# Attention on one core: the next image's pieces in other rounds, keys of two heads in one row tile, and the exponentials' sums right behind the scores

## The chip, the core and the metric

The kernel runs on one core of a Trainium2 chip. Its time is the device time of one launch in microseconds (us), here the median of several runs. The engines are TensorE (PE in the profile; its weight loads are PEld), VectorE (DVE), ScalarE (ACT), GpSimd (POOL) and SyncE (SP, which issues the DMAs). Each takes its own instructions in order and waits for others by semaphores. Matmuls write to PSUM; a PSUM tile of 128 x 512 float32 is called a bank here.

## What is computed

The whole is a block of two layers over eight images of 128 channels and 32 x 32 places: attention, a spectral filter, a deformable convolution and a mixture of experts, each behind a norm and added to its input. The change lies in the first of them, cut here to what matters:

```python
x = x + attention(layer_norm_over_channels(x), wq, wk, wv)      # 8 images
# in attention, per image: 1024 tokens of 128 channels, 8 heads of 16
q, k, v = (xp @ w.T for w in (wq, wk, wv))
weights = softmax(einsum('bhwnd,bxynd->bnhwxy', q, k) * 16 ** -0.5)
out = einsum('bnhwxy,bxynd->bhwnd', weights, v)
```

All is float32. The scores are bounded beforehand, so that the softmax needs no maximum: exponential, sum, division.

## The kernel before, in words

`metaformer_kernel` first prepares image 0 (`BoundedAttention.tokens` and `.matrices`) and then calls `attention_bounded`, lines 495 to 755, which does all eight images. The later stages (`Spectral`, `DeformAndExperts`) follow on the same engines; the change doesn't touch them.

**Units and rounds.** A unit is a quarter of an image's queries (256) with four of its eight heads (a head group, `hg`): eight units per image, 64 in all. A unit has four rounds `r`, and each round takes two of the eight key tiles. The work is written as a list of entries (round, order in the round, function), sorted, and issued in that order; each engine's queue is then the order of its own instructions in that list. A unit that begins at round `t0` is spread over twelve rounds, so that three units overlap:

- rounds `t0` to `t0+3`, order 0, `scores` (L596): eight matmuls (as the profile counts, 16 passes) of 32 rows by 128 columns, one for each head and key tile, into `s`, which takes four PSUM banks and has one buffer; then ScalarE's exponential of all of it into `e` (L609). Order 1, `add_tiles` (L615): GpSimd adds the two key tiles of `e` into `t`.
- round `t0+5`, order 4, `sums` (L621): matmuls with `group` add `t` over groups of partitions into `z`; order 5, `reciprocals` (L630) on VectorE.
- round `t0+6`, order 2.5, `spread_out` (L634): matmuls spread the reciprocals over the partitions again, into `rb`; rounds `t0+6` to `t0+9`, order 3, `divide` (L644): VectorE multiplies `e` by `rb`.
- rounds `t0+8` to `t0+11`, `values` (L650): matmuls with the values' tiles into `av`. The second tile is split between the end of `t0+8` and `t0+9`.
- every second unit: `take` (L664) copies `av`, and `results` (L668) turns it back with two matmuls by `pick`, copies it, and GpSimd adds it to the image's tokens `xt`.

Since units begin at rounds divisible by four, the same kinds of work meet in all rounds of one number modulo 4.

**The next image.** Between these stand the pieces that prepare the next image, by lists of round numbers (L698 to L731): `load` its channels, `tokens` (L533, transposes into `xt`), 25 pieces of the layer norm (`layer_norm_pieces`, L66: eight of statistics on VectorE, nine of the inverse deviation on GpSimd, two small operations each, eight normalisations on ScalarE into `ht`), `channels` (L543, transposes of `ht` into `hk`), and the projections: `keys` (L569) and `queries` (L555), one matmul of 128 x 512 for each head group and half image, and `key_values` (L582). All small matmul results, `z` among them, go through one PSUM bank (`small_bank`, L527), and ScalarE copies them out (VectorE reads `z`).

**Layout of the heads.** Head `4 hg + j` has row tile `j` (32 rows) of head group `hg`; its 16 channels fill the first half of the tile, the rest is zero, for queries and keys alike. So keys exist once for each head group.

The lists of rounds as they stand, for image 2 and later (`first` is the image's first round):

```python
project_at = [first + n for n in (-13, -12, -9, -5, -4, -1, 3, 4, 7, 11)]
turn = {"channels": (first - 20, first - 17)}
turn.update(load=first - 42, tokens=(first - 38, first - 34))
norm_at = [first - n for n in (
    37, 36, 35, 34, 33, 32, 32, 31, *range(31, 22, -1), 22, 22, 22, 21, 19, 19, 18, 18)]
```

Of the kernel before, what the change touches and what calls it, by code (L numbers as in the profile page):

```python
# [18 lines left out]
P = 128  # L19
# [380 lines left out]
class BoundedAttention:  # L400
# [6 lines left out]
    def __init__(self, nc, cp):  # L407
        self.nc = nc
        HG, NH = self.HG, self.NH
        self.xc = cp.tile([P, T], F32, name="xc")  # L410
        self.ht = cp.tile([P, NT, C], F32, name="ht")
        self.hk = cp.tile([P, T], F32, name="hk")
        self.wq, self.wk = (cp.tile([P, HG, NH, 32], F32, name=n) for n in ("wq", "wk"))
        self.wv = cp.tile([C, C], F32, name="wv")
        self.group = cp.tile([P, NG], F32, name="group")
        self.spread = cp.tile([P, 2, P], F32, name="spread")
        self.pick = cp.tile([P, HG, NH, HD], F32, name="pick")

    def keys_view(self):
        return self.hk.rearrange("c (r p) -> c r p", p=P)  # L420

    def tokens(self, x, ident, pool, ps):

        nc = self.nc
        nc.sync.dma_start(self.xc, x[0].rearrange("c h w -> c (h w)"))
        xv = self.xc.rearrange("c (i p two) -> c two i p", two=2, p=P)
        st = pool.tile([P, NT, 6], F32, name="f_st")
        mv = pool.tile([P, NT, 2], F32, name="f_mv")
        banks = []
        for par in range(2):  # L430
            pt = ps.tile([P, 4, P], F32, tag="x", name="p_x")
            for i in range(4):
                nc.tensor.transpose(pt[:, i, :], xv[:, par, i, :], ident)
            banks.append(pt)
            for i in range(4):
                nc.vector.bn_stats(st[:, 4 * par + i, :], pt[:, i, :])
                nc.vector.bn_aggr(mv[:, 4 * par + i, :], st[:, 4 * par + i, :])
        rs = inverse_std(nc, pool, mv[:, :, 1], 1e-6, nc.vector)
        for par in range(2):
            for i in range(4):  # L440
                n = 4 * par + i
                nc.vector.tensor_scalar(
                    self.ht[:, n, :], banks[par][:, i, :], mv[:, n, 0:1], rs[:, n : n + 1],
                    ALU.subtract, ALU.mult,
                )
# [3 lines left out]
            nc.scalar.copy(  # L449
                self.keys_view()[:, 4 * par : 4 * par + 4, :].rearrange(  # L450
                    "c r (g m) -> c r g m", m=4
                ),
                pb.rearrange("c i p -> c (i p)").rearrange("c (g r m) -> c r g m", r=4, m=4),
            )

    def matrices(self, wqT, wkT, wvT):
        nc, HG, NH = self.nc, self.HG, self.NH
        for w, src in ((self.wk, wkT), (self.wq, wqT)):
            nc.gpsimd.memset(w, 0.0)
            for hg in range(HG):  # L460
                nc.sync.dma_start(
                    w[:, hg, :, 0:HD],
                    src[:, hg * NH * HD : (hg + 1) * NH * HD].rearrange("c (h d) -> c h d", d=HD),
                )
        nc.sync.dma_start(self.wv, wvT)

        group = self.group
        nc.gpsimd.memset(group, 1.0)
# [15 lines left out]
            )  # L484


        nc.gpsimd.memset(self.pick, 0.0)
        for hg in range(HG):
            nc.gpsimd.affine_select(
                out=self.pick[:, hg], in_=self.pick[:, hg], pattern=[[-32, NH], [-1, HD]],  # L490
                base=-HD * hg, channel_multiplier=1, compare_op=ALU.not_equal, fill=1.0,
            )


def attention_bounded(ctx, tc, ident, x, x1d, given, weigh, head):


# [8 lines left out]
    QU = 256  # L506
    QC = T // QU
    UNITS = HG * QC
    wq, wk, wv = given.wq, given.wk, given.wv
    group, spread, pick = given.group, given.spread, given.pick  # L510
    hk = given.keys_view()
    cp = ctx.enter_context(tc.tile_pool(name="a_const", bufs=1))
    sb = ctx.enter_context(tc.tile_pool(name="a_sb", bufs=2))
    ep = ctx.enter_context(tc.tile_pool(name="a_e", bufs=11))
# [25 lines left out]
        xt = img["xt"][:, par * 4 : par * 4 + 4, :]  # L540
        nc.scalar.copy(xt.rearrange("p a c -> p (a c)"), pt)

    def channels(par):  # L543
# [6 lines left out]
        nc.scalar.copy(  # L550
            hk[:, 4 * par : 4 * par + 4, :].rearrange("c r (g m) -> c r g m", m=4),
            pt.rearrange("c (g r m) -> c r g m", r=4, m=4),
        )

    def queries(img, hg, par):  # L555
# [3 lines left out]
        nc.tensor.matmul(  # L559
            pq, wq[:, hg].rearrange("c h d -> c (h d)"),  # L560
            hk[:, 4 * par : 4 * par + 4, :].rearrange("c r p -> c (r p)"),
            start=True, stop=True,
        )
        nc.scalar.copy(
            img["q"][:, hg, par, :].rearrange("p (g r m) -> p r g m", r=4, m=4),
            pq.rearrange("p (r g m) -> p r g m", r=4, m=4),
        )

    def keys(img, hg, par):  # L569
        if "k" not in img:  # L570
            img["k"] = sb.tile([P, HG, NT, P], F32, tag="k", name="k")
        pk = small_bank("pk")
        nc.tensor.matmul(  # L573
            pk, wk[:, hg].rearrange("c h d -> c (h d)"),
            hk[:, 4 * par : 4 * par + 4, :].rearrange("c r p -> c (r p)"),
            start=True, stop=True,
        )
        nc.scalar.copy(
            img["k"][:, hg, 4 * par : 4 * par + 4, :].rearrange("p c n -> p (c n)"), pk
        )  # L580

    def key_values(b, img, par):  # L582
        pv = small_bank("pv")
        for r in range(4):
            nc.tensor.matmul(
                pv[:, r * P : (r + 1) * P], hk[:, 4 * par + r, :], wv,
                start=True, stop=True,
            )
        img["v"] = vts[b % 2]
# [6 lines left out]
    def scores(img, un, r):  # L596
# [4 lines left out]
        for c in range(2):  # L601
            for j in range(NH):
                rows = slice(32 * j, 32 * j + 32)
                nc.tensor.matmul(  # L604
                    s[:, j, c, :], img["k"][rows, hg, 2 * r + c, :],
                    q[rows, qc * QU : (qc + 1) * QU], start=True, stop=True,
                )
        e = ep.tile([P, NH, 2, QU], F32, tag="e", name="e")
# [59 lines left out]
    def results(b, img, qc, qrt):  # L668
# [1 line left out]
            img["at"] = sb.tile([P, NT, C], F32, tag="at", name="at", bufs=1)  # L670
        po = small_bank("po")
        for i in range(2):
            nc.tensor.matmul(  # L673
                po[:, i * P : (i + 1) * P], qrt["o"][:, i * P : (i + 1) * P],
                pick.rearrange("p g j d -> p (g j d)"), start=True, stop=True,
            )
        nc.scalar.copy(
            img["at"][:, 2 * qc : 2 * qc + 2, :].rearrange("p i c -> p (i c)"), po[:, 0 : 2 * P]
# [16 lines left out]
    for b in range(B):  # L695
        img = {}
        first = 4 * UNITS * b
        project = [  # L698
            (keys, img, 0, 0), (keys, img, 0, 1), (queries, img, 0, 0),
            (keys, img, 1, 0), (keys, img, 1, 1), (queries, img, 1, 0),  # L700
            (key_values, b, img, 0), (key_values, b, img, 1),
            (queries, img, 0, 1), (queries, img, 1, 1),
        ]
        if b == 0:
            turn = {"tokens": (0, 0)}
            project_at = (-1, -1, -1, 0, 1, 2, 3, 4, 7, 11)
        else:
            project_at = [first + n for n in (-13, -12, -9, -5, -4, -1, 3, 4, 7, 11)]
            turn = {"channels": (first - 20, first - 17)}
            if b == 1:  # L710
                turn.update(load=0, tokens=(2, 3))
                norm_at = (3, 3, 4, 4, 5, 5, 6, 6) + (6, 7, 7, 8, 8, 8, 9, 9, 9) + (
                    10, 10, 10, 11, 13, 13, 14, 14)
            else:
                turn.update(load=first - 42, tokens=(first - 38, first - 34))
                norm_at = [first - n for n in (
                    37, 36, 35, 34, 33, 32, 32, 31, *range(31, 22, -1), 22, 22, 22, 21, 19, 19, 18, 18
                )]
        if b:
            at(turn["load"], 6, load, b)  # L720
            spread_rounds(
                layer_norm_pieces(nc, sb, lambda i=img: i["xt"], lambda: given.ht, 1e-6), norm_at
            )
            for par in range(2):
                at(turn["channels"][par], 5.5, channels, par)
# [6 lines left out]
        for qc in range(QC):  # L732
            qrt = {}
            for hg in range(HG):
                un = {"at": (qc, hg)}
                t0 = first + 4 * (HG * qc + hg)
                for r in range(4):
                    at(t0 + r, 0, scores, img, un, r)
                    at(t0 + r, 1, add_tiles, un, r)
                    at(t0 + 5, 4, sums, un, r)  # L740
                    at(t0 + 6 + r, 3, divide, un, r)
                at(t0 + 8, 2, values, img, un, 0, (0, 1), qrt)
                at(t0 + 8, 6.5, values, img, un, 1, (0,), qrt)
                at(t0 + 9, 2, values, img, un, 1, (1,), qrt)
                at(t0 + 10, 2, values, img, un, 2, (0, 1), qrt)
                at(t0 + 11, 2, values, img, un, 3, (0, 1), qrt)
                at(t0 + 5, 5, reciprocals, un)
                at(t0 + 6, 2.5, spread_out, un)
# [1491 lines left out]
```

## Time and profile before

| | us |
|---|---|
| runs, median (lowest to highest of 3) | 1886.62 (1885.5 to 1890.1) |
| profiled execution | 1886.46 |
| its span | 1884.7 |
| busy: TensorE, VectorE, GpSimd, ScalarE over the span | 1682.4, 1389.0, 1157.9, 1064.8 |
| busy in the attention stage, 0 to 905 us: TensorE, VectorE, GpSimd, ScalarE | 863.5, 715.6, 665.7, 588.0 |
| one exponential (L609), 256 of them, mean | 1.88 |
| one division (L646), 256 of them, mean | 2.28 |
| one sum of two tiles (L618), 256 of them, mean | 2.38 |
| one reciprocal (L632), 64 of them, mean | 1.76 |

The profile is of one execution. In it, "busy" is the time in which an engine has an instruction under way; matmuls overlap with each other, so that a busy TensorE need not be at its peak. Behind an arrow stands the instruction that ended an engine's wait. The chain of waits is the work that ended last, followed backwards from the last instruction: it tells at each moment what the end of the whole was waiting for. A row's name is the tile that is written and, behind the arrow, the tiles that are read, with the line of the kernel.

### The profile page before, as it was taken

The page shows a single profiled execution, that of the slowest core. Times are in us where ns is not written, and L with a number is a line of the kernel's source. Part 1 is how long each engine was busy: PE and PEld are TensorE (multiplying, and loading weights), DVE is VectorE, ACT ScalarE, POOL GpSimd, SP SyncE. Part 2 cuts the span into 40 slices and gives each one's busy share as a digit, 9 for nine tenths or more (in the row PEclk, how much of TensorE's full clock was granted, in tenths as well). Part 3 has the DMA queues.
Part 4 walks back from the last instruction along what each step waited for, and adds up shares of the span by engine and source line. Part 5 has one row for each costly group of instructions (what it writes and reads, how often), then busy time and mean ns, then how long its engine had stood idle before and what let it go on. Part 6 is the DMA issues. An engine that isn't in the chain of part 4 may idle for free.

```text
span 1884.7 us, 51873 instructions
## 1 busy us (share of the span) xinstructions
PE 1682.4 (89%) x22324; PEld 1033.1 (55%) x22324; DVE 1389.0 (74%) x2107; ACT 1064.8 (56%) x1692; POOL 1157.9 (61%) x1219
## 2 busy tenths in 40 slices
PE   6899999999999999998577899999888497888788
PEld 3455555555555555554233688888665264555555
DVE  3688787878888888888544666666148888999883
ACT  3666666676766667666234455555145655666630
POOL 3778777777878777787221244345126768888740
PEclk9999999999999999999788999999899687999999
DMA  1000000000000000000658322122568775755620
GB/s 30 13 2 24 2 2 24 2 24 2 24 2 24 2 2 24 2 13 2 143 142 242 129 71 71 48 71 59 179 194 263 237 213 153 234 174 164 205 81 21
DMA packets 157998, 156.15 MB, mean 83 GB/s; under 512 B 15424, under 2 KB 136864, under 8 KB 156352
## 3 DMA queue, kind: packets, MB, share of 16 engines
q1 hardware_dynamic: 142400, 102.41, 19.1%
q0 software_dynamic: 15360, 50.34, 8.5%
q8 instruction: 176, 2.88, 0.6%
q14 instruction: 62, 0.51, 0.1%
HBM read 96.39 MB, written 56.33 MB: 81 GB/s over the span
## 4 chain that ended last, share of the span: by engine, by line
PE 60%; DVE 16%; issue 7%; POOL 6%; ACT 4%; DMA 2%; SPq 2%; DVEq 0%; ACTq 0%; POOLq 0%
PE s L604 14%; PE av L656 13%; PE p_g L1958 6%; PE z L625 6%; PE p_z L2007 5%; PE rb L639 4%; PE p_out L1420 3%; DVE ga L1410 3%; DVE g L1317 2%; ACT e L609 2%; PE pq L559 2%; PE pk L573 2%; POOL g L1295 1%; DVE zs L2019 1%; PE po L673 1%
## 5 line engine op out<-in xcount | busy, mean ns | idle before, releaser
L618 POOL TENSOR_TENSOR t<-e 128x1024 f32<-128x1024 f32 x256 | 608.2, 2376 | 204.7 <-ACT e L609 204.4
L646 DVE TENSOR_TENSOR e<-e,rb 128x2048 f32<-128x2048 f32 x256 | 570.4, 2278 | 84.5 <-PE rb L639 84.5
L609 ACT ACTIVATE e<-s 128x2048 f32<-128x2048 f32 x256 | 481.0, 1879 | 255.1 <-PE s L604 252.0
L604 PE MATMUL s<-q,k 32*128 32x256 f32 x4096 | 295.2, 402 | 14.6 <-ACT e L609 13.8
L656 PE MATMUL av<-e,vt 128*32 128x256 f32 x4096 | 287.4, 388 | 4.8 <-DVE e L646 3.5
L1295 POOL DMA_INDIRECT g<-tab,idx x192 | 200.3, 1043 | 134.1 <-ACT cn_m L1515 66.8
L604 PEld LDWEIGHTS s<-q,k 32*128 32x128 f32 x4096 | 185.9, 185 | 137.8 <-ACT e L609 116.9
L1302 ACT ACTIVATE g<-g,w 128x128 f32<-128x128 f32 x604 | 186.4, 390 | 57.0 <-DMA g<-tab,idx 43.2
L1983 POOL TENSOR_SCALAR at<-uc 128x256 f32<-128x256 f32 (+2 forms) x62 | 75.4, 1219 | 173.4 <-PE p_z L2007 128.9
L656 PEld LDWEIGHTS av<-e,vt 128*32 128x32 f32 x4096 | 101.1, 109 | 141.5 <-issue 83.8
L1958 PE MATMUL p_g<-v,a 32*128 32x128 f32 x4096 | 159.3, 284 | 9.4 <-ACT ga L1690 3.7
L632 DVE RECIPROCAL r<-z 128x256 f32<-128x256 f32 x64 | 112.5, 1758 | 70.4 <-PE z L625 70.2
L1958 PEld LDWEIGHTS p_g<-v,a 32*128 32x128 f32 x4096 | 132.3, 186 | 38.3 <-issue 23.0
L1420 PE MATMUL p_out<-ga,ew 128*128 128x512 f32 x256 | 127.5, 645 | 15.5 <-DVE ga L1410 15.4
L625 PE MATMUL z<-t,group 128*32 128x256 f32 x2048 | 122.2, 379 | 0.0
L1692 DVE COPY gb<-p_g 128x512 f32<-128x512 f32 x128 | 82.4, 685 | 46.7 <-PE p_g L1958 46.1
L1692 DVE COPY ga<-p_g 128x512 f32<-128x512 f32 x128 | 82.4, 686 | 44.0 <-PE p_g L1958 44.0
L1690 ACT COPY gb<-p_g 128x512 f32<-128x512 f32 x128 | 68.7, 589 | 69.6 <-PE p_g L1958 68.8
L1690 ACT COPY ga<-p_g 128x512 f32<-128x512 f32 x128 | 68.7, 589 | 66.7 <-PE p_g L1958 66.7
L1410 DVE TENSOR_TENSOR ga<-p_g,tc 128x2048 f32<-128x2048 f32 x32 | 73.0, 2282 | 29.5 <-PE p_g L1401 29.5
L1420 PEld LDWEIGHTS p_out<-ga,ew 128*128 128x128 f32 x256 | 50.1, 205 | 75.6 <-issue 56.2
L625 PEld LDWEIGHTS z<-t,group 128*32 128x32 f32 x2048 | 66.4, 110 | 44.1 <-issue 0.3
(312 smaller groups left out, 2421.3 us busy)
## 6 DMA issues: line engine op xcount, KB each, us to landing
tab<-hx SPq DMA_DIRECT2D x24, 512.0 KB, 5.8
tab<-hx SPq DMA_DIRECT2D x72, 128.0 KB, 5.3
ud<-us SPq DMA_DIRECT2D x8, 1024.0 KB, 5.3
uc<-ud SPq DMA_DIRECT2D x16, 512.0 KB, 4.0
yd<-zs SPq DMA_DIRECT2D x32, 256.0 KB, 3.2
ga<-yd SPq DMA_DIRECT2D x32, 256.0 KB, 3.8
xc<-in_x SPq DMA_DIRECT2D x8, 512.0 KB, 3.9
x1d<-xt SPq DMA_DIRECT2D x8, 512.0 KB, 2.9
```

The costliest lines, as they stand in the source:

```text
L604: nc.tensor.matmul(s[:, j, c, :], img["k"][rows, hg, 2 * r + c, :], q[rows, qc * QU : (qc + 1) * QU], start=True, stop=True,)
L609: nc.scalar.activation(e.rearrange("p j c q -> p (j c q)"), s.rearrange("p j c q -> p (j c q)"), AF.Exp, scale=float(HD) ** -0.5,)
L618: nc.gpsimd.tensor_add(t, e[:, :, 0, :], e[:, :, 1, :])
L625: nc.tensor.matmul(un["z"][32 * j : 32 * j + 32, 0:QU], group, un["t", r][:, j, :], start=(r == 0), stop=(r == 3), skip_group_check=True,)
L646: nc.vector.tensor_tensor(e, e, un["rb"].unsqueeze(2).to_broadcast([P, NH, 2, QU]), ALU.mult)
L656: nc.tensor.matmul(qrt["av"][32 * j : 32 * j + 32, 0:QU], img["v"][:, 2 * r + c, P * hg + 32 * j : P * hg + 32 * j + 32], un["e", r][:, j, ...
L1295: nc.gpsimd.indirect_dma_start(out=t["g", i][:, tap].rearrange("p k c -> p (k c)"), out_offset=None, in_=rows, in_offset=bass.IndirectOffs ...
L1302: nc.scalar.activation(t["g", i][:, tap, k, :], t["g", i][:, tap, k, :], AF.Identity, scale=t["w"][:, i, tap, k : k + 1],)
L1420: nc.tensor.matmul(t["out"], self.ew[:, first + e, :], xg[:, e, :], start=(first + e == 0), stop=(first + e == NE - 1), skip_group_check=True,
L1690: self.nc.scalar.copy(dst, src)
L1692: self.nc.vector.tensor_copy(dst, src)
L1958: nc.tensor.matmul(banks[j][:, i * P : (i + 1) * P], self.a[rows, 4 * n + i, :], self.v[rows, ch].rearrange("p f k -> p (f k)"), start=Tru ...
```

## The change

It does five things, all in the attention stage.

1. Heads are laid out in another way: head `2 j + hg` has row tile `j`. A row tile of the keys now holds two heads, 16 rows each, and serves both head groups; the queries of head group `hg` keep zeros in the other head's rows. There is one key projection for half an image instead of two, and the key tile is half as large. The values' matrix is reordered in the same way, and since the results then come out in the order of the channels, `results` uses transposes by the identity instead of matmuls by `pick`, which goes.
2. `hk`, the turned channels, has two buffers, taken in turn by image.
3. `sums` goes from order 4 to order 1.5 of its round: behind the scores, ahead of values, spread and divisions.
4. The second half of the second value tile goes from round `t0+9` to `t0+10`, ahead of `spread_out`; the third value tile goes behind `spread_out` (order 2.7).
5. The pieces of the next image go to other rounds. All projections now lie in rounds of number 3 modulo 4, tokens, channels and results in those of number 0 (with exceptions in images 0 and 1), the statistics in those of number 1, and the inverse deviation is done in four rounds with two or three pieces each.

```diff
-        self.hk = cp.tile([P, T], F32, name="hk")
-        self.wq, self.wk = (cp.tile([P, HG, NH, 32], F32, name=n) for n in ("wq", "wk"))
-        self.wv = cp.tile([C, C], F32, name="wv")
+        self.hk = [cp.tile([P, T], F32, name=f"hk{n}") for n in range(2)]
+        self.wq = cp.tile([P, HG, NH, 32], F32, name="wq")
+        self.wk = cp.tile([C, C], F32, name="wk")
+        self.wv = cp.tile([C, HG, NH, HD], F32, name="wv")
...
-        for w, src in ((self.wk, wkT), (self.wq, wqT)):
-            nc.gpsimd.memset(w, 0.0)
-            for hg in range(HG):
-                nc.sync.dma_start(
-                    w[:, hg, :, 0:HD],
-                    src[:, hg * NH * HD : (hg + 1) * NH * HD].rearrange("c (h d) -> c h d", d=HD),
-                )
-        nc.sync.dma_start(self.wv, wvT)
+        nc.sync.dma_start(self.wk, wkT)
+        nc.gpsimd.memset(self.wq, 0.0)
+        for hg in range(HG):
+            at = slice(HD * hg, HD * hg + HD)
+            nc.sync.dma_start(
+                self.wq[:, hg, :, at], wqT.rearrange("c (h n) -> c h n", n=2 * HD)[:, :, at]
+            )
+            nc.sync.dma_start(
+                self.wv[:, hg], wvT.rearrange("c (h n) -> c h n", n=2 * HD)[:, :, at]
+            )
...
-        nc.gpsimd.memset(self.pick, 0.0)
-        for hg in range(HG):
-            nc.gpsimd.affine_select(
-                out=self.pick[:, hg], in_=self.pick[:, hg], pattern=[[-32, NH], [-1, HD]],
-                base=-HD * hg, channel_multiplier=1, compare_op=ALU.not_equal, fill=1.0,
-            )
...
-    def keys(img, hg, par):
+    def keys(b, img, par):
         if "k" not in img:
-            img["k"] = sb.tile([P, HG, NT, P], F32, tag="k", name="k")
+            img["k"] = sb.tile([P, NT, P], F32, tag="k", name="k")
...
-                    s[:, j, c, :], img["k"][rows, hg, 2 * r + c, :],
+                    s[:, j, c, :], img["k"][rows, 2 * r + c, :],
...
-            nc.tensor.matmul(
-                po[:, i * P : (i + 1) * P], qrt["o"][:, i * P : (i + 1) * P],
-                pick.rearrange("p g j d -> p (g j d)"), start=True, stop=True,
+            nc.tensor.transpose(
+                po[:, i * P : (i + 1) * P], qrt["o"][:, i * P : (i + 1) * P], ident
             )
...
         project = [
-            (keys, img, 0, 0), (keys, img, 0, 1), (queries, img, 0, 0),
-            (keys, img, 1, 0), (keys, img, 1, 1), (queries, img, 1, 0),
+            (keys, b, img, 0), (keys, b, img, 1), (queries, b, img, 0, 0), (queries, b, img, 1, 0),
             (key_values, b, img, 0), (key_values, b, img, 1),
-            (queries, img, 0, 1), (queries, img, 1, 1),
+            (queries, b, img, 0, 1), (queries, b, img, 1, 1),
         ]
+        project_at = [first + n for n in (-13, -9, -5, -1, 3, 7, 11, 15)]
         if b == 0:
             turn = {"tokens": (0, 0)}
-            project_at = (-1, -1, -1, 0, 1, 2, 3, 4, 7, 11)
+            project_at = (-1, -1, -1, 3, 4, 7, 11, 15)
+        elif b == 1:
+            turn = {"load": 0, "tokens": (8, 12), "channels": (18, 20)}
+            norm_at = (9, 9, 10, 10, 13, 13, 14, 14) + (14, 14, 15, 15, 15, 15, 16, 16, 16) + (
+                17, 17, 17, 17, 18, 18, 19, 19)
         else:
...
+            turn = {
+                "load": first - 42, "tokens": (first - 36, first - 28),
+                "channels": (first - 20, first - 12),
+            }
+            norm_at = [first - n for n in (35, 35, 31, 31, 27, 27, 27, 27)] + [
+                first - n for n in (26, 26, 25, 25, 24, 24, 23, 23, 23)
+            ] + [first - n for n in (22, 22, 21, 21, 19, 18, 15, 14)]
...
-                    at(t0 + 5, 4, sums, un, r)
+                    at(t0 + 5, 1.5, sums, un, r)
                     at(t0 + 6 + r, 3, divide, un, r)
                 at(t0 + 8, 2, values, img, un, 0, (0, 1), qrt)
                 at(t0 + 8, 6.5, values, img, un, 1, (0,), qrt)
-                at(t0 + 9, 2, values, img, un, 1, (1,), qrt)
-                at(t0 + 10, 2, values, img, un, 2, (0, 1), qrt)
+                at(t0 + 10, 2, values, img, un, 1, (1,), qrt)
+                at(t0 + 10, 2.7, values, img, un, 2, (0, 1), qrt)
```

More of the change, by code (lines that the diff above doesn't have):

```diff
@@ L411, in __init__, with keys_view @@
         self.ht = cp.tile([P, NT, C], F32, name="ht")
-        self.hk = cp.tile([P, T], F32, name="hk")
-        self.wq, self.wk = (cp.tile([P, HG, NH, 32], F32, name=n) for n in ("wq", "wk"))
-        self.wv = cp.tile([C, C], F32, name="wv")
+        self.hk = [cp.tile([P, T], F32, name=f"hk{n}") for n in range(2)]
+        self.wq = cp.tile([P, HG, NH, 32], F32, name="wq")
+        self.wk = cp.tile([C, C], F32, name="wk")
+        self.wv = cp.tile([C, HG, NH, HD], F32, name="wv")
         self.group = cp.tile([P, NG], F32, name="group")
         self.spread = cp.tile([P, 2, P], F32, name="spread")
-        self.pick = cp.tile([P, HG, NH, HD], F32, name="pick")
-    def keys_view(self):
-        return self.hk.rearrange("c (r p) -> c r p", p=P)
+    def keys_view(self, b):
+        return self.hk[b % 2].rearrange("c (r p) -> c r p", p=P)
     def tokens(self, x, ident, pool, ps):
@@ L449, in tokens @@
             nc.scalar.copy(
-                self.keys_view()[:, 4 * par : 4 * par + 4, :].rearrange(
+                self.keys_view(0)[:, 4 * par : 4 * par + 4, :].rearrange(
                     "c r (g m) -> c r g m", m=4
@@ L508, in attention_bounded @@
     UNITS = HG * QC
-    wq, wk, wv = given.wq, given.wk, given.wv
-    group, spread, pick = given.group, given.spread, given.pick
-    hk = given.keys_view()
+    wq, wk, wv = given.wq, given.wk, given.wv.rearrange("c g j d -> c (g j d)")
+    group, spread = given.group, given.spread
     cp = ctx.enter_context(tc.tile_pool(name="a_const", bufs=1))
@@ L541, in tokens, with channels @@
         nc.scalar.copy(xt.rearrange("p a c -> p (a c)"), pt)
-    def channels(par):
+    def channels(b, par):
         pt = small_bank("pb")
@@ L550, in channels, with queries @@
         nc.scalar.copy(
-            hk[:, 4 * par : 4 * par + 4, :].rearrange("c r (g m) -> c r g m", m=4),
+            given.keys_view(b)[:, 4 * par : 4 * par + 4, :].rearrange(
+                "c r (g m) -> c r g m", m=4
+            ),
             pt.rearrange("c (g r m) -> c r g m", r=4, m=4),
         )
-    def queries(img, hg, par):
+    def queries(b, img, hg, par):
         if "q" not in img:
@@ L560, in queries @@
             pq, wq[:, hg].rearrange("c h d -> c (h d)"),
-            hk[:, 4 * par : 4 * par + 4, :].rearrange("c r p -> c (r p)"),
+            given.keys_view(b)[:, 4 * par : 4 * par + 4, :].rearrange("c r p -> c (r p)"),
             start=True, stop=True,
@@ L567, in queries @@
         )
[L569 removed]
+    def keys(b, img, par):
         if "k" not in img:
[L571 removed]
+            img["k"] = sb.tile([P, NT, P], F32, tag="k", name="k")
         pk = small_bank("pk")
         nc.tensor.matmul(
[L574 to L575 removed]
+            pk, wk, given.keys_view(b)[:, 4 * par : 4 * par + 4, :].rearrange("c r p -> c (r p)"),
             start=True, stop=True,
@@ L578, in keys @@
         nc.scalar.copy(
-            img["k"][:, hg, 4 * par : 4 * par + 4, :].rearrange("p c n -> p (c n)"), pk
+            img["k"][:, 4 * par : 4 * par + 4, :].rearrange("p c n -> p (c n)"), pk
         )
@@ L585, in key_values @@
             nc.tensor.matmul(
-                pv[:, r * P : (r + 1) * P], hk[:, 4 * par + r, :], wv,
+                pv[:, r * P : (r + 1) * P], given.keys_view(b)[:, 4 * par + r, :], wv,
                 start=True, stop=True,
@@ L698, in attention_bounded @@
         project = [
-            (keys, img, 0, 0), (keys, img, 0, 1), (queries, img, 0, 0),
-            (keys, img, 1, 0), (keys, img, 1, 1), (queries, img, 1, 0),
+            (keys, b, img, 0), (keys, b, img, 1), (queries, b, img, 0, 0), (queries, b, img, 1, 0),
             (key_values, b, img, 0), (key_values, b, img, 1),
-            (queries, img, 0, 1), (queries, img, 1, 1),
+            (queries, b, img, 0, 1), (queries, b, img, 1, 1),
         ]
+        project_at = [first + n for n in (-13, -9, -5, -1, 3, 7, 11, 15)]
         if b == 0:
             turn = {"tokens": (0, 0)}
-            project_at = (-1, -1, -1, 0, 1, 2, 3, 4, 7, 11)
-        else:
[L708 to L718, printed above, removed]
+            project_at = (-1, -1, -1, 3, 4, 7, 11, 15)
[3 more added lines that the diff above has]
+                17, 17, 17, 17, 18, 18, 19, 19)
+        else:
+            turn = {
[5 more added lines that the diff above has]
+            ] + [first - n for n in (22, 22, 21, 21, 19, 18, 15, 14)]
         if b:
@@ L724, in attention_bounded @@
             for par in range(2):
-                at(turn["channels"][par], 5.5, channels, par)
+                at(turn["channels"][par], 5.5, channels, b, par)
         for par in range(2):
```

## Prediction

> **What bounds the kernel now.** I read the page's slices first, then the busy time by stage, then the chain of waits round by round, then the order of time on all engines. The change touches only the attention stage, which runs from 0 to about 905 us; behind it the order of instructions on every engine is the same in both kernels, so the rest is taken as unchanged. By stage, TensorE is busy 109.5 of every 110 us between 160 and 820 us (clock 1.00), VectorE 91, GpSimd 85, ScalarE 75. That looks like a plain TensorE bound, but the chain says more. Its columns are start, length, what:
>
> ```profile
> 415.41 1.07 PE s L604 x16
> 416.48 0.57 PE av L656 x8
> 417.05 1.73 PE z L625 x32
> 418.78 1.08 PE s L604 x16
> 419.86 1.00 PE av L656 x16
> 420.86 1.06 PE rb L639 x8
> 421.92 1.13 PE s L604 x16
> 423.05 1.00 PE av L656 x16
> 424.05 1.05 PE pk L573 x2
> 425.11 1.09 PE s L604 x16
> 426.19 1.00 PE av L656 x16
> 427.19 1.05 PE pk L573 x2
> 428.25 0.57 PE av L656 x8
> ```
>
> These are four rounds, one unit's period. Call them by their number modulo 4: round 1 (scores, half of the second value tile, sums) takes 3.37 us, round 2 (scores, values, spread reciprocals) 3.14, round 3 (scores, values, a projection) 3.19, round 0 (scores, values, a piece, half a value tile) 3.71. Every scores group is followed at once by other matmuls. What happens where TensorE has less to do stands near the end of the last image, which has no projections:
>
> ```profile
> 850.14 1.15 PE L604 MATMUL s<-q,k 32*128 32x256 f32 x16 [1.00 <-ACT e L609]
> ...
> 851.38 1.88 ACT L609 ACTIVATE e<-s 128x2048 f32<-128x2048 f32 x1 [0.92 <-PE s L604]
> ...
> 853.31 1.15 PE L604 MATMUL s<-q,k 32*128 32x256 f32 x16 [0.59 <-ACT e L609]
> ```
>
> Scores have one buffer of four PSUM banks. The exponential starts 1.24 us after its scores, takes 1.88, and the next scores start 0.05 later: 3.17 us is a floor of every round, set by the loop scores, exponential, scores. So a round takes the larger of 3.17 us and its TensorE work, and slack of one round can't be carried into the next, since TensorE is in order and the next scores wait for this exponential. This decides the case: TensorE work taken from a round above 3.17 counts, taken from one at 3.17 it doesn't, and moved into a round already full it costs all of it.
>
> Check on before: round 0 with results 3.30 (four an image), with keys 3.73 (two), with values' projection 3.74, with turned channels 3.25, sum 27.65; round 1, 8 x 3.38 = 27.0; round 2, 6 x 3.17 + 2 x 3.81 (with the next image's tokens) = 26.6; round 3, 8 x 3.17 = 25.4. Total 106.65; measured from scores to scores at the same place of two images (276.30 to 382.90 us) 106.6.
>
> **The change part by part, one image in the middle.**
> Round 1 loses the half value tile: 1.07 + 1.73 = 2.8 us of work, so 3.17 by the floor: 8 x (3.17 - 3.38) = -1.7.
> Round 2 gains it: scores 1.07, half tile 0.57, spread 1.06, values 1.00: 3.70 us of TensorE work against 3.14. Spread must also wait for the reciprocal. At the start the trace shows sums right behind scores, as the change makes them everywhere:
>
> ```profile
> 55.13 1.15 PE L604 MATMUL s<-q,k 32*128 32x256 f32 x16 [0.94 <-ACT e L609]
> ...
> 58.21 1.76 DVE L632 RECIPROCAL r<-z 128x256 f32<-128x256 f32 x1 [10.34 <-PE z L625]
> ...
> 60.02 0.73 PEld L639 LDWEIGHTS rb<-r,spread 64*128 64x128 f32 x8 [0.95 <-DVE r L632]
> ```
>
> That is 4.89 us from round 1's scores to spread; minus the round's 3.17 it is 1.72 into round 2, where TensorE is ready at 1.64. So 3.70 us if the wait vanishes, 3.78 if not; I take 3.78, since this is the very sequence. 8 x (3.78 - 3.17) = +4.9, and -1.3 more for the two tokens that leave round 2 (3.81 to the other rounds' 3.17).
> A rule weighs on this part. The Trainium skill ("TensorEngine Tiling (Array Packing)", Key Properties) says that a change of tiling mode drains TensorE. The rows agree in kind: eight value matmuls cost 0.57 and sixteen 1.00, not twice 0.50. The new round 2 goes scores, values, spread, values, scores: one mode change more than before per unit. By pure count the half tile would be 0.50 and the round 3.63 (0.07 x 64 = 4.5 us less in the whole); I keep the rows, which hold the drain.
> Round 0: results become transposes. The chain has four turned-channel transposes at 0.59, so two take about 0.3, where two matmuls with the pick matrix took 0.64; 2.94 us of work, so 3.17: 4 x -0.13 = -0.5. Keys and values' projection move out: 2 x -0.56 and -0.57, minus 1.7. Tokens (0.68) move in, 1.07 + 1.00 + 0.68 + 0.57 = 3.32 twice: +0.3; turned channels 3.24 twice (one came from round 3): +0.1.
> Round 3 carries all eight projections, 1.07 + 1.00 + 1.05 = 3.12, under the floor: nothing. Two of four key projections (1.05 us and a copy of 0.59 each) are gone from the image, but they are worth only what is counted in round 0.
> Sum: 12.7 + 6.64 + 6.48 (round 0), 25.36, 30.24, 25.36 = 106.8 against 106.6: +0.15. The 3.5 us less TensorE work is eaten by round 2.
>
> **Norm pieces on GpSimd.** Before, the inverse deviation was spread one piece of two small operations per round. Now it is two, two, two and three pieces in rounds 26 to 23 before the image, and ScalarE's first two normalisations stand in round 22 before it, in ScalarE's queue ahead of round 21's exponential. GpSimd has the tile sum of each round (2.38) and these behind it. From the start of the image the price is seen: a tile sum with four operations repeats in 3.35 us, with a residual add in 3.08, with both about 4.1. With round 26's scores at 0, tile sums start at 3.8, 7.1, 10.5 and (residual add in round 24) 14.5; then 2.35 and five operations 1.43 (74.76 to 76.19 us in the trace): ready at 18.3. ScalarE would start the exponential at 17.0 + 1.24 = 18.3, but has to do two normalisations first (0.8): 0.9 late, straight into the loop. The trace shows such a wait once (the exponential behind it began at 77.36, 1.2 after the normalisations):
>
> ```profile
> 76.19 1.26 ACT L105 ACTIVATE ht<-xt,lp_nm,lp_y 128x128 f32<-128x128 f32 x3 [1.87 <-POOL lp_nm L99]
> ```
>
> From below it costs nothing, if GpSimd is a microsecond quicker than I add up; from above 1.5. I take 0.9. Round 21 has a query copy and two normalisations (0.59 + 0.87, with the hand-over, against 1.24 of room): 0.25, of which before had some 0.1 in other rounds. Together +1.05, six images with +0.15: 6 x 1.2 = +7.
>
> **First image.** Key copies and projections leave rounds 0 and 1: round 1's scores start after the second token transposes, at 35.8 instead of 38.47. Here a rule speaks against the change: the skill ("TensorE: Matmul & The Clock Gate", Part 1) says that TensorE runs at half clock until it has been busy for some 3.4 us. The rows show it (scores 2.09 at 30 and 38 us, 1.15 from 42.58, behind 4.1 us without a gap; the granted clock doesn't show it). The lighter rounds 1 and 2 leave gaps, so I let them stay slow up to round 3: 4.1 us each instead of 3.17. Then round 5's scores are at 51.9 instead of 55.13 (at 50 if warm at once), round 12's, without today's wait of 1.9, at 74.9 instead of 79.27. The second image's inverse then falls in rounds 14 to 16 with eight operations in one: ready 3.0 us after round 17's exponential, and with four normalisations round 18's is 3.3 late; 0.6 of it lies beside round 2's longer work. Rounds 12 to 31: 66.8 + 2.7 + 0.3 = 69.8 against 67.2. Net -1.7.
> **Last image.** No projection to save: 8 x 3.17 x 3 + 8 x 3.78 = 106.3 against 104.0 (784.85 to 888.9): +2.3.
>
> At nothing: the second buffer of turned channels, the smaller key tile, the weight loads (as many transfers as before, done by 10 us, first needed at 21.8) and the dropped memset, pick and selects on GpSimd (done by 7 us; their cover is the flag at 20 us). The small bank is copied out some 0.4 us before the earlier sums want it (ScalarE needs 0.37 to 0.59 behind round 0's exponential, sums come 1.07 into round 1); sums' last tile sum is 1.8 us old. VectorE: divisions from 3.0 us into round 2 last 8.9, the next sums end at about 13.1; statistics lie in the gap of spread.
>
> Sum: -1.7 + 7 + 2.3 = +7.6 on the profiled execution's 1886.46 us (span 1884.7 and 1.8 around it; 0.2 under the median 1886.62): 1894.
>
> **Rivals.**
> 1. Likeliest (0.55): as worked out, 1894, own range 1888 to 1901.
> 2. Round 2 is long, but normalisation isn't late (GpSimd quicker, or scales in time): less 5.4 + 1.5 + some of the start, 1886, no change (0.20). For it: GpSimd is idle 0.3 to 0.8 us a round now. Against: the wait of 1.87 above, with fewer operations in a round.
> 3. Faster (0.15): TensorE's total rules, because slack does carry over. Then an image is 106.6 - 2.1 (keys) - 1.4 (results) = 103.1, and 7.5 of them give -26: 1860. It decides if scores can start before the exponential ends; for it speaks 109.5 busy of 110, against it the last image's waits of 0.6 to 1.0 for the exponential.
> 4. Much slower (0.10): the spread's wait grows, since statistics, reciprocal and divisions make VectorE's period (8.9 + 1.76 + 1.4 + up to 1.8 = 13.8) longer than the unit's 13.3; 0.3 a unit more, 64 units: 1913.
>
> Faster, same, slower by 0.3% (about what a measurement of this kernel can tell): below 1881, to 1892.3, above. Rival 3 and a tail of 2 give 0.17; rival 2's rest and the lower third of 1 give 0.32; the rest is 0.51. Range 1880 to 1904: it leaves out most of rivals 3 and 4.
>
> **What would show it.** Rounds by scores to scores: 3.17, 3.17, 3.78, 3.17. GpSimd's last small operation should release ScalarE's normalisation once an image with idle time ahead of it. Image period near 107.8, last image 106.3, round 5 at 50 to 52 us. Wrong if round 2 stays under 3.5 us, or if other rounds fall below 3.17.

## The result, and the profile after

The changed kernel takes 1893.58 us (median of 14 runs, 1887.55 to 1901.79), the kernel before 1886.70 in the same sessions (14 runs): ratio 1.003, 95% interval 1.0016 to 1.0045. So it is slower by 6.9 us, 0.3%. The profiled execution took 1899.01 us with a span of 1897.2: it is one of the longer ones, while the profiled execution of the kernel before (1886.46) lies at the median.

Lengths below are read from the start of one exponential to the next, in the order of time of ScalarE. An image runs from its first exponential to the first of the next image:

| us | before | changed |
|---|---|---|
| first exponential starts at | 32.3 | 31.3 |
| image 0 | 115.4 | 114.4 |
| images 1 to 5, each | 106.6 | 107.8 |
| image 6 | 105.3 | 107.6 |
| image 7 (31 rounds) | 100.8 | 103.3 |
| round 0, 1, 2, 3 modulo 4, median over images 2 to 6 | 3.33, 3.37, 3.19, 3.17 | 3.21, 3.17, 3.82, 3.17 |
| last exponential starts at | 886.9 | 895.4 |

The last exponential starts 8.6 us later. The first one had started 1.0 us earlier, which is not the change's doing: it starts at 32.1 to 32.3 us in every other profile, in those of kernels with the same beginning too. From first to last exponential the stage is 9.6 us longer. The rest of the span is 1001.8 us against 997.9; the instructions there are the same in the same order, and over the profiles of this study it lies between 994 and 1003.5 with no clear relation to the change (1041 to 1046.5 on one chip that was slower for every kernel), so those 4 us are taken as scatter.

The chain of waits of the changed kernel, one unit, rounds 2, 3, 0 and 1 and the next spread (start, length, what; `pk` is a key projection, `pb` turned channels, `z` the sums, `r` the reciprocals, `rb` their spread):

```profile
312.76 1.15 PE s L598 x16
313.91 0.57 PE av L650 x8
314.48 1.12 PE rb L633 x8
315.60 1.00 PE av L650 x16
316.60 1.08 PE s L598 x16
317.67 1.00 PE av L650 x16
318.68 1.06 PE pk L568 x2
319.73 1.11 PE s L598 x16
320.84 1.00 PE av L650 x16
321.84 0.59 PE pb L540 x4
322.43 0.57 PE av L650 x8
323.00 1.08 PE s L598 x16
324.07 1.93 PE z L619 x32
326.01 0.02 issue
326.03 1.77 DVE r L626
327.80 0.04 issue
327.84 1.13 PE rb L633 x8
```

Before, round 1 held scores, half a value tile and sums, and in the unit that the prediction shows the chain never left TensorE. Now the half tile stands in round 2 (313.91), which takes 3.84 us, and in round 1 the chain goes from the sums over VectorE's reciprocal straight to the spread: the exponential of round 1 isn't even on it, and the spread waits for the reciprocal. The page says the same in one line, where the idle time ahead of the reciprocal was 70.4 us before:

```profile
L626 DVE RECIPROCAL r<-z 128x256 f32<-128x256 f32 x64 | 112.5, 1758 | 116.3 <-PE z L619 116.3
```

Once an image the chain leaves TensorE for GpSimd. In the order of time, around the start of the first normalisation of an image:

```profile
286.55 1.88 ACT L603 ACTIVATE e<-s 128x2048 f32<-128x2048 f32 x1 [1.29 <-PE s L598]
...
289.94 0.24 POOL L99 TENSOR_SCALAR lp_nm<-lp_nm 128x8 f32<-128x8 f32 x1
...
290.21 0.88 ACT L105 ACTIVATE ht<-xt,lp_nm,lp_y 128x128 f32<-128x128 f32 x2 [1.78 <-POOL lp_nm L99]
...
290.99 1.85 ACT L603 ACTIVATE e<-s 128x2048 f32<-128x2048 f32 x1
```

From exponential to exponential these are 4.44 us, where the other rounds 2 take 3.82. ScalarE stood still for 1.78 us with its next exponential queued behind the normalisation, and that exponential is 0.6 us late.

### The profile page after: what moved, and what is told of

Its sections match the earlier page's. It is cut to its first block, busy times and chain, and to the rows that moved or that the text cites. A ratio compares the mean times of both kernels' runs of the same rounds, so it can differ in the third digit from the quotient of the medians.

```text
span 1897.2 us, 51680 instructions
## 1 busy us (share of the span) xinstructions
PE 1682.0 (89%) x22228; PEld 1017.0 (54%) x22228; DVE 1391.0 (73%) x2107; ACT 1052.2 (55%) x1676; POOL 1155.6 (61%) x1215
## 4 chain that ended last, share of the span: by engine, by line
PE 51%; DVE 16%; ACT 13%; issue 8%; POOL 7%; DMA 3%; SPq 2%; DVEq 0%; ACTq 0%; POOLq 0%
PE s L598 13%; ACT e L603 9%; PE av L650 9%; PE p_g L1951 7%; PE p_z L2000 5%; PE rb L633 4%; DVE ga L1403 3%; PE p_out L1413 2%; PE z L619 2%; DVE r L626 2%; DVE g L1310 2%; POOL g L1288 2%; PE pq L554 1%; DMA g<-tab,idx 1%; PE p_mix L1245 1%
## 5 line engine op out<-in xcount | busy, mean ns | idle before, releaser
L619 PEld LDWEIGHTS z<-t,group 128*32 128x32 f32 x2048 | 60.2, 109 | 54.2 <-issue 21.0
```

Source lines behind the costliest of these rows:

```text
L619: nc.tensor.matmul(un["z"][32 * j : 32 * j + 32, 0:QU], group, un["t", r][:, j, :], start=(r == 0), stop=(r == 3), skip_group_check=True,)
```

## The experiments

Each kernel is compared with the kernel before on the same chip. The last five ran on two other chips; on that of e5 to e8 the kernel before took 1933 us, so that only ratios and the lengths in the attention stage are compared.

**e1_half_back.** From the changed kernel:

```diff
-                at(t0 + 10, 2, values, img, un, 1, (1,), qrt)
-                at(t0 + 10, 2.7, values, img, un, 2, (0, 1), qrt)
+                at(t0 + 9, 2, values, img, un, 1, (1,), qrt)
+                at(t0 + 10, 2, values, img, un, 2, (0, 1), qrt)
```

> The changed kernel, with the second half of the second value tile back in round 1 (behind the sums) and the third value tile ahead of spread again; all else as changed. Theory (a round takes the larger of 3.17 us and its TensorE work): round 1 goes from 3.17 to about 3.37, round 2 from 3.82 to 3.17, -0.45 x 64 = -29 us; GpSimd then has shorter rounds to hide its small operations in and is later by about 0.5 us an image, +3; about 1868 us where the changed kernel has 1894. Rival (TensorE's total work sets the time, which is the same in both): no change, 1894.

Measured 1878.34 us against 1885.81, ratio 0.9963 (0.9946 to 0.9979), the last exponential at 876.1 instead of 895.4. Chain of waits, rounds 1 and 2:

```profile
306.21 1.15 PE s L598 x16
307.36 1.86 PE z L619 x32
309.22 0.43 PE av L650 x8
309.65 1.08 PE s L598 x16
310.73 1.00 PE av L650 x16
311.73 1.06 PE rb L633 x8
312.79 1.10 PE s L598 x16
```

Round 1 is at 3.37, round 2 at 3.17, as the theory said. The matmuls are the same, but the profile has TensorE busy for 103.3 us of an image instead of 105.2, so this run alone doesn't exclude that its total decides; e2 and e3 do.

The whole is 10 us short of the forecast. Some 5 of these lie in the stage, which is 20.3 us shorter than the changed kernel's where 26 was worked out. GpSimd's wait grew more than I allowed: the round with the late normalisation takes 4.6 us, 1.43 over the floor, where in the changed kernel it was 0.63 over its 3.82, so that the long round 2 had been hiding 0.8 us of it, 5 us in six images where I had put 3. And image 0 holds rounds of 7.4 and 4.8 (6.4 and 3.1 in the changed kernel). The other 5 us don't show in the stage and are not explained.

**e2_half_moved_alone.** The kernel before with the same two lines as the changed kernel has them.

> The kernel before, with only the half value tile moved from round 1 to round 2 and the third value tile behind spread. Theory: round 1 from 3.37 to 3.17, round 2 from 3.17 to 3.8 (from 3.81 to 4.45 where it also holds tokens), +0.42 x 64 = +27 us, 1913. Rival (TensorE's total): no change, 1887.

Measured 1910.95 us against 1885.81, ratio 1.0137 (1.0115 to 1.0159), +25 us by the medians. Round 1 went to 3.17, round 2 to 3.81, and to 4.46 where it holds tokens. Chain of waits, one round 2 and the start of the next scores:

```profile
306.63 1.15 PE s L604 x16
307.77 0.57 PE av L656 x8
308.34 0.03 issue
308.37 1.13 PE rb L639 x8
309.51 1.00 PE av L656 x16
310.51 1.20 PE s L604 x16
```

An image takes 3.6 us more (110.2 for 106.6). Again TensorE's busy time isn't quite the same, 108.1 us for 106.1; so 2.0 of the 3.6 are busy time, and 1.6 are time in which it now stands idle. This one move costs more than the whole change.

**e3_keys_alone.** The kernel before with the new layout of heads (tiles, matrices, keys, results), one buffer of turned channels, and

```diff
-            project_at = (-1, -1, -1, 0, 1, 2, 3, 4, 7, 11)
+            project_at = (-1, -1, -1, 2, 3, 4, 7, 11)
...
-            project_at = [first + n for n in (-13, -12, -9, -5, -4, -1, 3, 4, 7, 11)]
+            project_at = [first + n for n in (-13, -5, -9, -1, 3, 4, 7, 11)]
```

> The kernel before, with only the new layout of the heads: keys of two heads in one row tile (two key projections instead of four per image, in rounds 3 modulo 4) and results by transposes. One buffer of turned channels; rounds of the norm, tokens, sums and value tiles as before. Theory: the two rounds that held a key projection at round 0 fall from 3.72 to 3.17, the four with results from 3.3 to 3.17: -1.6 us an image, seven images; in image 0 the rounds 0 and 1 lose a projection and a copy each, -3; together about -13, 1873. Rival (TensorE's total): 2.1 + 1.4 us per image, -26, 1860.

Measured 1877.39 us against 1885.81, ratio 0.9947 (0.9926 to 0.9968). An image takes 105.1 instead of 106.6 us, -1.55 where -1.6 was worked out. TensorE's busy time in an image fell by 3.1 us, from 106.1 to 103.1 (the expectation counted 3.5), and its idle time rose from 0.5 to 2.0: half of what was taken away is lost at the floor. The round that the prediction shows at 425.11 us, 3.71 long with a key projection, is now:

```profile
421.72 1.18 PE s L598 x16
422.90 0.02 issue
422.93 1.89 ACT e L603
424.81 0.04 issue
424.86 1.15 PE s L598 x16
```

It takes 3.14 us, and the chain goes through the exponential. Image 0 hardly gains (115.2 for 115.4): its third round takes 6.6 us, where tokens, their copy, a query projection and the next scores follow each other, and TensorE stays slow longer: the scores at 46.39 and 52.07 us took 2.09 and 2.05, where before they took 1.15 from 42.58 on.

**e4_add_on_vector.** From the changed kernel:

```diff
-        nc.gpsimd.tensor_add(mine[0], mine[0], mine[1])
+        (nc.vector if qc == QC - 1 else nc.gpsimd).tensor_add(mine[0], mine[0], mine[1])
```

> The changed kernel, with the residual add of each image's last quarter on VectorE instead of GpSimd; it is the add that stands among the small operations of the next image's inverse deviation. Theory (ScalarE waits for GpSimd's last small operation once an image, and its next exponential is 0.65 us late): GpSimd is done 0.7 us earlier, the round of 4.45 us falls to 3.8, six images, -4 us; 1890. Rival (that round is long for ScalarE's own queue, two normalisations and a copy): no change. The round's length in the profile decides, more than the time.

Measured 1899.95 us against 1885.81, ratio 1.0077 (1.006 to 1.0094): slower than the changed kernel (1.003), though in the stage by some 2 us only. The round in question did fall, from 4.45 to 4.07 in five of the six images, so GpSimd is the cause of that wait; but in images 2 and 7 the same round rose to 5.74 and 5.95 (in image 7 from 3.84, as it prepares no next image). In the order of time, an image of the first kind and image 2:

```profile
392.59 0.43 DVE L674 TENSOR_TENSOR xt<-xt,at 128x256 f32<-128x256 f32 x1 [0.57 <-ACT at L670]
392.60 2.68 POOL L612 TENSOR_TENSOR t<-e 128x1024 f32<-128x1024 f32 x1
...
283.38 2.37 POOL L612 TENSOR_TENSOR t<-e 128x1024 f32<-128x1024 f32 x1
283.39 2.64 DVE L674 TENSOR_TENSOR xt<-xt,at 128x256 f32<-128x256 f32 x1 [0.56 <-ACT at L670]
```

When VectorE is first by 0.01 us, its add takes 0.43 and GpSimd's sum 0.3 longer than its 2.38, which takes back part of the 0.7 that GpSimd was to win: 4.07 and not 3.8. When GpSimd is first, VectorE's add ends 0.28 after GpSimd's sum, and divisions, reciprocal and spread behind it are late. The Trainium skill ("SBUF — State Buffer", Who interferes with whom) says that a VectorE instruction with two SBUF inputs contends with a GpSimd instruction that reads SBUF; the two rows agree. The divisions, with one input from PSUM, show no such wait: all 256 of the changed kernel take 2.25 to 2.29.

**e5_sums_alone.** The kernel before with `sums` at order 1.5.

> The kernel before, with only the sums right behind the scores (order 1.5 instead of 4); the half value tile stays in round 1, now behind the sums. Theory (a round takes the larger of 3.17 us and its TensorE work): the work of round 1 stays the same, 3.37 us, so nothing moves, 1886 give or take 2. Rival (the spread is held up by reciprocals that come late, and sums earlier by half a microsecond let it start earlier): round 2 gets shorter, up to 0.1 x 64 = 6 us less, 1880.

Measured 1934.93 us against 1933.46, ratio 1.0002 (0.9989 to 1.0014), images 1 to 5 at 106.6, as before, and round 2 at 3.17. The sums' place by itself does nothing.

**e6_spread_last.** The changed kernel with the third value tile at order 2.2.

> The changed kernel, with the third value tile ahead of spread (order 2.2 instead of 2.7); the half tile stays in round 2. Theory (part of round 2's 3.82 us is TensorE waiting for the reciprocal): with 1 us of work ahead of the spread the wait goes, round 2 falls to about 3.72, 0.1 x 64 = 6 us less, 1888. Against it: divisions start 0.9 us later in their unit, and VectorE has only about 1 us of room before the next reciprocal; if that is used up, round 2 or the next round 1 grows and nothing is won.

Measured 1932.52 us against 1933.46, ratio 0.9995 (0.9981 to 1.0008); an image takes 106.1 instead of 107.8. Chain of waits, one round 2:

```profile
311.74 1.15 PE s L598 x16
312.88 1.43 PE av L650 x24
314.31 1.06 PE rb L633 x8
315.38 1.08 PE s L598 x16
```

Round 2 is 3.57, not the 3.72 expected: besides the wait, the two value groups now stand together, 1.43 instead of 0.57 + 1.00, so the cut itself had cost 0.14. VectorE had the room: rounds 1 stayed at 3.17.

**e7_inverse_early.** From e1_half_back, four buffers of `xt` instead of three and, for images 2 and later:

```diff
-                "load": first - 42, "tokens": (first - 36, first - 28),
+                "load": first - 66, "tokens": (first - 60, first - 36),
...
-            norm_at = [first - n for n in (35, 35, 31, 31, 27, 27, 27, 27)] + [
-                first - n for n in (26, 26, 25, 25, 24, 24, 23, 23, 23)
-            ] + [first - n for n in (22, 22, 21, 21, 19, 18, 15, 14)]
+            norm_at = [first - n for n in (59, 59, 55, 55, 35, 35, 35, 35)] + [
+                first - n for n in range(34, 25, -1)
+            ] + [first - n for n in (23, 23, 22, 22, 19, 18, 15, 14)]
+            if b == 2:
+                turn.update(load=14, tokens=(24, 28))
+                norm_at[0:4] = 4 * [25]
```

> The changed kernel with the half tile back in round 1 (as in e1_half_back), and with the next image's tokens and statistics earlier (60 and 36 rounds ahead, four buffers of tokens), so that the inverse deviation is done in nine rounds, one piece each, from 34 to 26 rounds ahead. Theory (in e1_half_back ScalarE waits for GpSimd once an image, and that round takes 4.6 us instead of 3.17): the wait goes, 1.4 us for each of six images, -8; 1870 where e1_half_back had 1878, 1886 the kernel before. Rival (the long round comes from ScalarE's own normalisations and copies): no change.

Measured 1920.97 us against 1933.46, ratio 0.9931 (0.991 to 0.9952). The round of 4.6 us is 3.2, an image takes 103.8 instead of 105.0, so the wait was GpSimd's. Image 0 rose to 117.0 (113.8 in e1_half_back). Of these 3.2 us, 1.4 lie in round 24, where the third image's tokens share the small bank with results; 1.0 in round 3, as TensorE was slow for one round more; and 0.8 in rounds 18 and 19. Ahead of round 18's exponential ScalarE waits 3.95 us for GpSimd, and behind that wait the granted clock was 0.50 from 101 to 106 us, with scores of 2.09 at 102.01.

**e8_split_half.** From e7_inverse_early (`values` also takes a list of heads):

```diff
+                if hg == 0:
+                    at(t0 + 8, 6.6, values, img, un, 1, (1,), qrt, (0, 1))
-                at(t0 + 9, 2, values, img, un, 1, (1,), qrt)
+                at(t0 + 9, 2, values, img, un, 1, (1,), qrt, range(2 if hg == 0 else 0, 4))
```

> e7_inverse_early, and the half value tile of units with the first head group cut once more: two heads' matmuls at the end of round 0 (which then has 3.2 us of TensorE work, beside results), two in round 1. Theory: 32 rounds fall from 3.37 to 3.17, -0.2 x 32 = -6 us; 1864. Rival (TensorE's total): no change, or slightly more for one more change of shape.

Measured 1923.17 us against 1933.46, ratio 0.9942 (0.992 to 0.9965), an image 104.8 instead of 103.8: a miss. Chain of waits, a round 0 with results and the round 1 behind it:

```profile
488.51 1.00 PE av L650 x16
489.51 0.37 PE po L667 x2
489.88 0.99 PE av L650 x12
490.86 1.08 PE s L598 x16
491.94 1.86 PE z L619 x32
493.80 0.43 PE av L650 x4
494.23 1.08 PE s L598 x16
```

Four passes for two heads take 0.43, as eight for four heads did in e1_half_back, and twelve take 0.99, as sixteen do. The four heads' matmuls write side by side into four column tiles of 32; leaving two of them out saved no time. Round 0 grew by 0.25 and round 1 did not shrink.

**e9_image0.** From e7_inverse_early:

```diff
-            turn = {"load": 0, "tokens": (8, 12), "channels": (18, 20)}
-            norm_at = (9, 9, 10, 10, 13, 13, 14, 14) + (14, 14, 15, 15, 15, 15, 16, 16, 16) + (
-                17, 17, 17, 17, 18, 18, 19, 19)
+            turn = {"load": 0, "tokens": (2, 8), "channels": (18, 20)}
+            norm_at = (3, 3, 3, 3, 9, 9, 9, 9) + (10, 10, 11, 11, 12, 13, 14, 14, 15) + (
+                16, 16, 17, 17, 18, 18, 19, 19)
...
-                turn.update(load=14, tokens=(24, 28))
+                turn.update(load=14, tokens=(22, 28))
```

> e7_inverse_early, with the second image's pieces earlier in image 0 (tokens in rounds 2 and 8, statistics in 3 and 9, inverse deviation in rounds 10 to 15) and the third image's first tokens in round 22 instead of 24, where they shared the one small bank with results. Theory: image 0, 117.0 us in e7_inverse_early with rounds of 7.4, 4.1, 4.6 and 4.6 us, loses these waits and takes about 111; 6 us less, ratio to the kernel before 0.990 where e7_inverse_early had 0.993. Rival (image 0 is bound by the slow start of TensorE and by its copies, the long rounds only take the place of other waits): no change.

Measured 1867.89 us against 1884.33, ratio 0.9911 (0.9887 to 0.9935); image 0 takes 110.4, so the rival falls, and the last exponential starts at 865.0. The late round 17 is 3.37 where it was 7.39, and the granted clock stays at 1.00 from 60 to 120 us. This version beats both kernels.

## Why the prediction was right

The forecast was 1894.0 us and a slower kernel; measured 1893.6. The steps:

- **The rule of the round** (the larger of 3.17 us and TensorE's work, nothing carried over) holds in the rounds that wait for nothing else, in both kernels and in e1, e2, e3 and e5. The plainest case is e3: TensorE's busy time falls by 3.1 us per image, the image by the 1.55 that lay in rounds above the floor. In e2 the same matmuls in another order cost 3.6 us an image with 2.0 more of busy time. Rival 3 (TensorE's total, 1860) is out.
- **Rounds as forecast:** 3.17, 3.17, 3.78, 3.17 worked out, 3.21, 3.17, 3.82, 3.17 measured. Of round 2, the half tile is most, and the wait for the reciprocal plus the cut of the value group in two the rest: e6 takes away 0.25 by both. Of those 0.14 is the cut (1.57 against 1.43), the drain that the prediction kept by the rows, and 0.1 the wait, of which it had 0.08.
- **Late normalisation:** the mechanism was right, shown by the wait of 1.78 us, by e4's shorter round where its add went first, and by e7. The size was put at 0.9 and is 0.63, by three differences of about 0.1 each that all point one way. Counted from round 26's scores as in the prediction, in the image whose rows stand above (290.21 us): GpSimd is done at 18.2, not 18.3; the exponential was due at 18.4, not 18.3, since the rounds in between were a little longer; and the two normalisations with the hand-over take 0.8, not 0.9. The start of the first tile sum was wrong by more (3.8 worked out, 3.26 measured, when the exponential ends), but nothing came of it: the second sum waits for its own exponential and starts at 7.0, where 7.1 was worked out. The query copy with two normalisations was put at 0.25 and costs at most 0.1 (rounds of 3.17 to 3.24).
- **Images in the middle:** +1.2 forecast, +1.13 measured, with two errors that cancel: round 2 was longer, normalisation earlier.
- **Image 6** was counted as one in the middle. Before, it had no tokens of a next image and took 105.3, so the change cost 2.3 there, not 1.2. The last image: +2.3 forecast, +2.5 measured.
- **First image:** here the agreement is luck. Round 5's scores were put at 51.9 us and start at 51.82. But the first scores began 1.0 us early in this execution (29.12, in all others 30.0 to 30.1), and TensorE stayed slow through round 4, where the prediction said round 3, which took 1.0 us more. From the order of time of the changed kernel:

```profile
42.94 2.09 PE L598 MATMUL s<-q,k 32*128 32x256 f32 x16 [2.00 <-ACT e L603]
...
47.71 2.09 PE L598 MATMUL s<-q,k 32*128 32x256 f32 x16 [0.67 <-ACT q L559]
...
51.82 1.15 PE L598 MATMUL s<-q,k 32*128 32x256 f32 x16
```

In e1 and e6, with the same order of work up to here, the scores of round 4 took 1.15 (48.52 us in e1); in e4, e7 and e8 they took 2.09. So both happen with the same work, and the prediction's rule of some 3.4 us doesn't decide between them.

The late exponential of round 18 was put at 3.3 us; it comes 6.39 us after that of round 17 instead of 3.17, 3.2 late. From its first exponential on, image 0 is 1.0 us shorter; -1.7 was worked out.
- **Sums ahead of the values** were counted at nothing by themselves: e5 agrees. That they let the chain run over the reciprocal to the spread only matters once the half tile has left round 1.
- **The whole:** +7.6 us worked out, +6.9 measured by the medians, +9.6 in the profiled stage from first to last exponential. Part by part the stage has -1.0 for the first image (-1.7 forecast), +5.7 for images 1 to 5 (+6.0), +2.3 for image 6 (+1.2) and +2.5 for the last (+2.3). The sign, the place and the size are earned; that the sum meets the median to 0.4 us is luck.

What stays open: the 4 us behind the attention stage in the profiled execution are called scatter because the profiles differ by as much without a reason in the code; no run tests it. Nor is it certain that a change in the stage arrives whole at the end. By the medians the whole moved less than the profiled stage for the changed kernel and in four experiments: -7 us for -11 in e1, +25 for +28 in e2, -8 for -10 in e3, -16 for -22 in e9. In e4 it moved more, +14 for +12.

## What to carry to other kernels

Where one buffer ties two engines into a loop (scores, exponential, scores), count work per turn of the loop, not per engine: work taken from a turn that is above the loop's floor is worth all of it, from one at the floor nothing, and moving it between turns can cost more than a whole saving elsewhere, here 25 us for half a tile against 8 us won by fewer projections. A small operation on a slow engine comes onto the path when an instruction that waits for it stands in front of the loop's own instruction in some queue; spread such pieces one per turn. Four heads' matmuls that run side by side are one piece of work: cut them by key tile, not by head.

## What was not expected of the hardware

- Two of four column tiles take the same 0.43 us as four (e8), and twelve passes 0.99 as sixteen 1.00.
- Value groups next to each other cost less than apart: 24 passes 1.43, against 0.57 + 1.00 with a spread between them (e6); behind the sums, with tiles of the same shape, eight passes cost 0.43 (e1).
- An add of 128 x 256 on VectorE took 0.43 us when it began 0.01 ahead of GpSimd's sum and 2.64 when it began 0.01 behind (e4).
- TensorE stayed at half speed though it had been busy from 42.94 to 47.04 us: after a gap of 0.67 the scores at 47.71 still took 2.09. In e1, behind the same sequence, they took 1.15.
- TensorE also fell back to half speed in the middle of a kernel: in e7 it stood idle for 1.04 and then 1.32 us between 98 and 102 us, and the granted clock was 0.50 from 101 to 106 us. A long wait in image 0 so cost more than its own length.
- The recorded clock of the first 50 us is 0.64 in the profile of the changed kernel and 1.00 in the one of before, whose scores took 2.09 us as well, at 30.07 and 38.47.
